# Layer 3's mixing emitted in thirteen shorter steps per group beside the states; narrow heads' turn and division a step apart

## Chip, cores and metric

One Trainium2 chip, one of its cores. The metric is the device time of one execution in microseconds (us), the median of the runs shown. Five engines work side by side, each with an in-order queue of its own: TensorE (PE in the profile, its weight loads PEld), VectorE (DVE), ScalarE (ACT), GpSimd (POOL) and SyncE (SP, which only issues transfers).

## What is computed

The reference is a graph network of four layers over 3125 nodes of 256 features and 50,000 edges. Each layer adds a message-passing block, a mixing block over all nodes and a feed-forward block to x. Three of these matter here, cut to their core:

```python
# layer 2, first graph attention (4 heads of 64), and layer 3's local attention (4 heads of 64)
w = exp(leaky_relu(s[src] + d[dst]) - bound[dst])
out = segment_sum(xW[src] * w, dst) / segment_sum(w, dst)      # then bias, elu, W2 (layer 2)

# layer 3, states: 256 channels x 16 states, nodes in an order by degree
h_t = dA_t * h_(t-1) + dBx_t ;  y_t = sum over states (h_t * C_t)   # then + x*D, * silu(z), @ out_proj

# layer 3, mixing: linear attention of 8 heads, then a small network
msg = layernorm((Q @ KV / (Q @ sumK)) @ Wm)
x + layernorm(relu(concat(x, msg) @ W1) @ W2)                 # W1: 512 x 512, W2: 512 x 256
```

All are 32-bit floats.

## The kernel before

Nodes are cut into 25 tiles of 125. The kernel is one Python class that emits instructions; many of its methods are generators, and a caller advances one generator a step (up to its next `yield`) in order to place its instructions among those of another. The recording layer then lays the instructions out on each engine's queue in an order near to that of emission, but not the same: independent instructions of neighbouring steps are interleaved.

**Narrow heads** (`sums_by_feature`, L1154; called for layer 2's first attention and for layer 3's local attention). Target tiles are taken in four blocks of 7, 6, 6 and 6 tiles (`COLUMNS`, L58). In a block, for each of the 25 source tiles s, a tile of the adjacency is loaded, VectorE makes one product t of 125 x 750 for each of 4 heads (L1209; 875 wide in the first block), and TensorE adds features x t to the sums: L1214 for the numerators, two heads side by side in the two halves of PE's 128 columns, in two chunks of 375; L1223 for the denominators, four heads in groups of 32 columns, emitted for two source tiles at a time. The sums fill six PSUM banks and two more (pool `gf_ps`) are left for everything else. After a block ScalarE copies the sums out (L1231), and each target tile becomes a job (`tile_work`, L1169): TensorE turns its sums with three transposes into `ps_sum` (L1173), and `use` divides them on VectorE (`shares`, L1243 to L1247), adds a bias and applies elu (L1287 to L1291). In layer 2 (`use1`, L1310) further steps turn the tile (x2t, L1318) and multiply it by W2 (ps_h, L166 by way of `product`); in layer 3 (`use`, L1909) the elu ends it. `advance` (L1180), called after every second source tile of the next block, moves every active job by one step, the oldest first, and starts one waiting job. So transposes and division of a tile are emitted in one step. After the last block a loop advances until no job is left.

**States with mixing beside** (`l3_mamba`, L1952). Nodes go in seven groups (`GROUPS`, L57): six of 4 tiles (500 nodes) and one of 1. For each group there are 16 states, and for each state and each half of the channels a fixed chain (`recur`, L2066): TensorE spreads a row of B over the partitions (ps_b, L2073), ScalarE makes da (L2080), VectorE multiplies u by ps_b (L2081) and runs the scan over the 500 nodes (L2082), GpSimd multiplies the result by a row of C (L2085), and TensorE adds it to y through an identity (L2091). State s+1 is emitted ahead of the sum of state s-1. Among the states stand, one step per state, the next group's preparation (`first_part`: input projection, convolution, softplus) and, for the first nine states of a group, one step of `beside`, which is the mixing (`l3_mix`, L1835) together with a search for a maximum (`peak`) whose first 16 steps ride on the mixing's. What is left of `beside` is run out after the last group.

The mixing goes over the same seven groups with weights that are loaded before. A group of 4 tiles takes eight steps: queries; heads; turn; product with Wm; centring; scaled turn; the hidden layer (four chunks, each four matmuls of 500 columns and one Relu on ScalarE); the product with W2 (four tiles, each four matmuls of 256 columns, and a copy on ScalarE). What follows the last one (second centring, gain, sum into X on GpSimd) goes with the next group's first step. The mixing and `peak` have two PSUM banks (pool `m3_ps`), the states the other six. The hidden layer and the outward product are emitted by the helpers `hidden` (L552) and `outward` (L565), which other blocks of the kernel use too.

The slots of a group:

```python
                    if s:
                        next(more, None)
                    if s % 16 < 9:
                        next(beside, None)
```

Of the kernel before, what the change touches and what calls it, by code (L numbers as in the profile page):

```python
# [60 lines left out]
class Net:  # L61
# [487 lines left out]
        nc.scalar.activation(m, m, AF.Exp)  # L549
        nc.vector.scalar_tensor_tensor(out, x, 0.0, m, op0=ALU.max, op1=ALU.add)  # L550

    def hidden(self, psum, out, w1, xt, chunks, func, bias=None, scale=None):  # L552

        nt = xt[0].shape[-1]
        for f in range(chunks):
            ps = psum.tile([128, 512], F32, name="ps_hidden", tag="mm")
            self.product(ps[:, :nt], [w1[:, k, f * 128:(f + 1) * 128] for k in range(len(xt))], xt)
            kw = {}
            if bias is not None:
                kw["bias"] = bias[:, f:f + 1]  # L560
            if scale is not None:
                kw["scale"] = scale[:, f:f + 1]
            self.nc.scalar.activation(out[:, f, :], ps[:, :nt], func, **kw)  # L563

    def outward(self, psum, ht, w2, chunks, n, use, bias=None):  # L565

        for j0 in range(0, n, 2):
            ps = psum.tile([128, 512], F32, name="ps_out", tag="mm")
            for j in range(j0, min(j0 + 2, n)):
                y = ps[:P, (j - j0) * D:(j - j0 + 1) * D]  # L570
                self.product(y, [ht[:, k, j * P:(j + 1) * P] for k in range(chunks)]
                             + ([] if bias is None else [self.ones[:, :P]]),
                             [w2[:, k, :] for k in range(chunks)] + ([] if bias is None else [bias]))
            for j in range(j0, min(j0 + 2, n)):
                use(j, ps[:P, (j - j0) * D:(j - j0 + 1) * D])

    def attention_keys(self, wp, prefix, xnt, biased, banks):

# [575 lines left out]
    def sums_by_feature(self, es, mine, over, h, heads, width, loops, use):  # L1154

        nc = self.nc
        pairs = heads // 2  # L1160
        most = max(n for _, n in COLUMNS) * P
        lp = es.enter_context(self.pool("gf_p", heads + 1))
        ap = es.enter_context(self.pool("gf_a", 4))
        tp = es.enter_context(self.pool("gf_t", 3 * heads + 1))
        op = es.enter_context(self.pool("gf_o", 1))
        cp = es.enter_context(self.pool("gf_acc", 1, PSUM))
        pp = es.enter_context(self.pool("gf_ps", 2, PSUM))

        def tile_work(sums, j, i):  # L1169
            js = slice(j * P, (j + 1) * P)  # L1170
            ps = pp.tile([128, 512], F32, name="ps_sum", tag="mm")
            for k in range(pairs + 1):
                nc.tensor.transpose(ps[:P, k * 128:(k + 1) * 128], sums[:, k, js], self.ident)  # L1173
            num = ps[:P, :heads * width].rearrange("p (h c) -> p h c", h=heads)
            den = ps[:P, heads * width:heads * width + 128].rearrange("p (h c) -> p h c", h=heads)[:, :, 0]
            yield from use(pp, i, (num, den), None) or ()

        waiting, active = [], []

        def advance():  # L1180
            for job in list(active):
                if next(job, self) is self:
                    active.remove(job)
            if waiting:
                job = waiting.pop(0)
                if next(job, self) is not self:
                    active.append(job)

        for i0, n in COLUMNS:
            w = n * P  # L1190
            chunks = ((0, (n + 1) // 2 * P), ((n + 1) // 2 * P, w))
            rows = []
            for hd in range(heads):
                rows.append(lp.tile([P, most], F32, name="rows"))
                self.spread(pp, [(rows[hd][:, b0 * P:b1 * P].rearrange("p (n q) -> p n q", q=P),
                                  [mine[:, i0 + j, hd:hd + 1] for j in range(b0, b1)])
                                 for b0, b1 in ((0, (n + 1) // 2), ((n + 1) // 2, n))])
            acc = [[cp.tile([128, 512], F32, name=f"acc{k}{c}") for c in range(2)] for k in range(pairs + 1)]
            held = []
            for s in range(NT):  # L1200
                a = ap.tile([P, most], F32, name="a")
                self.halves(nc.sync, a[:, :w], self.adj_rows()[s * P:(s + 1) * P, i0 * P:i0 * P + w])
                if loops and i0 <= s < i0 + n:
                    blk = a[:, (s - i0) * P:(s - i0 + 1) * P]
                    nc.vector.tensor_add(blk, blk, self.ident[:P, :P])
                t = []
                for hd in range(heads):
                    t.append(tp.tile([P, most], F32, name="t"))
                    nc.vector.scalar_tensor_tensor(t[hd][:, :w], rows[hd][:, :w], over[:, s, hd:hd + 1],  # L1209
                                                   a[:, :w], op0=ALU.max, op1=ALU.mult)  # L1210
                for k in range(pairs):
                    for c, (c0, c1) in enumerate(chunks):
                        for q in range(2):
                            nc.tensor.matmul(acc[k][c][q * width:(q + 1) * width, :c1 - c0],  # L1214
                                             h[:, s, 2 * k + q, :width], t[2 * k + q][:, c0:c1],
                                             start=(s == 0), stop=(s == NT - 1), skip_group_check=True)
                held.append((s, t))
                if s % 2 == 0 and s < NT - 1:
                    continue
                for s1, t1 in held:  # L1220
                    for c, (c0, c1) in enumerate(chunks):
                        for hd in range(heads):
                            nc.tensor.matmul(acc[pairs][c][hd * 32:(hd + 1) * 32, :c1 - c0],  # L1223
                                             h[:, s1, hd, width:].to_broadcast([P, 32]), t1[hd][:, c0:c1],
                                             start=(s1 == 0), stop=(s1 == NT - 1), skip_group_check=True)
                held = []
                advance()
            sums = op.tile([128, pairs + 1, most], F32, name="sums")
            for k in range(pairs + 1):
                for c, (c0, c1) in enumerate(chunks):  # L1230
                    nc.scalar.copy(sums[:, k, c0:c1], acc[k][c][:, :c1 - c0])  # L1231
            waiting += [tile_work(sums, j, i0 + j) for j in range(n)]
        while waiting or active:
            advance()
# [600 lines left out]
    def l3_mix(self, weights, kvs, pp, xt):  # L1835
# [3 lines left out]
        with ExitStack() as es:  # L1839
            kp = es.enter_context(self.pool("m3"))  # L1840
            for g, n in GROUPS:
                w = n * P
                x = kp.tile([128, KC, 4 * P], F32, name="x")
                nc.sync.dma_start(x[:, :, :w], xt[:, :, g * P:g * P + w])
                xs = [x[:, c, :w] for c in range(KC)]
                att = yield from self.attention_queries(kp, pp, xs, wq, None, kvs, n)
                yield
                y = kp.tile([P, 4, D], F32, name="y")

                def keep(j, ps):  # L1850
                    nc.scalar.copy(y[:, j, :], ps)
                self.outward(pp, att, wm, KC, n, keep)
                yield
                msg = kp.tile([P, 4, D], F32, name="heads")
                self.centred(kp, msg[:, :n, :], y[:, :n, :], n, "n1")
                yield
                mt = kp.tile([128, KC, 4 * P], F32, name="att")
                self.turn_scaled(pp, mt[:, :, :w], msg[:, :n, :], n, g1, c1)
                yield
                h = kp.tile([128, 4, 4 * P], F32, name="h")  # L1860
                self.hidden(pp, h[:, :, :w], w1, xs + [mt[:, c, :w] for c in range(KC)], 4, AF.Relu)
                yield
                self.outward(pp, h, w2, 4, n, keep)
                yield
                msg = kp.tile([P, 4, D], F32, name="heads")
                self.centred(kp, msg[:, :n, :], y[:, :n, :], n, "n2")
                nc.vector.tensor_mul(msg[:, :n, :], msg[:, :n, :], g2[:, None, :].to_broadcast([P, n, D]))
                nc.gpsimd.tensor_add(self.X[:, g:g + n, :], self.X[:, g:g + n, :], msg[:, :n, :])
# [83 lines left out]
    def l3_mamba(self, xs, ys, beside):  # L1952
# [6 lines left out]
        with ExitStack() as es:  # L1959
# [151 lines left out]
            for k, (g, n) in enumerate(GROUPS):  # L2111
# [8 lines left out]
                for s in range(S):  # L2120
# [5 lines left out]
                        next(done, None)  # L2126
                    if s:
                        next(more, None)
                    if s % 16 < 9:
                        next(beside, None)  # L2130
                self.through(more)
                add(S - 1, w, acc, terms[S - 1])
# [433 lines left out]
```

## Time and profile before

| what | us |
|---|---|
| median of 3 runs (6839.69 to 6856.35) | 6845.12 |
| the profiled execution | 6837.53 |
| its span, first to last instruction | 6835.7 |
| layer 2's narrow heads, first sum to last | 3736.1 to 4237.7 |
| states with mixing, first scan to last scan's end | 4986.3 to 5645.1 |
| layer 3's narrow heads, first sum to last | 5675.0 to 6223.5 |

Mean granted TensorE clock over the span: 0.911 of full speed. In the profile, "busy" is the time in which an engine had an instruction in work; a row of a group gives the line, the engine, what it writes and reads, count, busy time, the mean of one, and the engine's idle time ahead of it with what ended it. One fp32 matmul of the program shows as two TensorE instructions ("passes"), one of bf16 as one. Busy tenths of VectorE and TensorE's granted clock over the span, 171 us a digit (the states' stage is digits 30 to 33, the narrow heads 22 to 25 and 34 to 37):

```profile
DVE  7634123216777744115046887546478787776433
```

```profile
PEclk9887998998899999889967999989889988998887
```

### The profile page before, as it was taken

What the parts mean: (1) busy time and instruction counts of PE and PEld (TensorE: products, weight loads), DVE (VectorE), ACT (ScalarE), POOL (GpSimd) and SP (SyncE); (2) the same over time, 40 slices, a digit from 0 to 9 for tenths busy, and PEclk for the clock granted to TensorE, in tenths of its full rate; (3) what the DMA queues carried; (4) which work ended last, traced back from release to release, by engine and by line L of the source; (5) the groups of instructions that cost most, each with busy time, mean ns of one, the idle gap of its engine ahead of it and who ended that gap; (6) DMA issues with size and microseconds to landing.
All of it is one profiled execution on the core that took longest, in us unless ns stands there. A gap on an engine that the chain in (4) does not pass through costs nothing. (4 is left out here: it accounts for less than half of the span.)

```text
span 6835.7 us, 78438 instructions
## 1 busy us (share of the span) xinstructions
PE 5895.7 (86%) x29487; PEld 3956.4 (58%) x29487; DVE 3703.1 (54%) x7628; ACT 1607.7 (24%) x3404; POOL 890.0 (13%) x685
## 2 busy tenths in 40 slices
PE   6887899997799989899946999989778878997775
PEld 5555785564799978668833344776434443333553
DVE  7634123216777744115046887546478787776433
ACT  2433002232011110123323011002356660003411
POOL 0000000003100001400041000120344441001111
PEclk9887998998899999889967999989889988998887
DMA  2634447401122234225510221430331223222132
GB/s 67 107 48 65 120 134 218 139 10 56 54 61 65 60 110 135 63 83 171 167 46 25 79 80 56 138 102 1 92 49 49 53 48 95 65 70 72 43 116 76
DMA packets 421340, 562.01 MB, mean 82 GB/s; under 512 B 120485, under 2 KB 307169, under 8 KB 417153
## 3 DMA queue, kind: packets, MB, share of 16 engines
q1 hardware_dynamic: 353687, 458.72, 25.3%
q10 hardware_dynamic: 40467, 70.52, 3.7%
q0 software_dynamic: 26752, 27.20, 1.5%
q8 instruction: 247, 4.05, 0.2%
q14 instruction: 187, 1.53, 0.1%
HBM read 446.41 MB, written 109.65 MB: 81 GB/s over the span
## 5 line engine op out<-in xcount | busy, mean ns | idle before, releaser
L1134 DVE SCALAR_TENSOR_TENSOR t<-rows,over,a 125x625 f32<-125x625 f32 x750 | 619.7, 866 | 424.3 <-PE acc L1139 417.1
L1209 DVE SCALAR_TENSOR_TENSOR t<-rows,over,a 125x750 f32<-125x750 f32 (+1 forms) x800 | 794.7, 1044 | 56.5 <-PE acc L1223 52.0
L1214 PE MATMUL acc<-t,g_h 125*64 125x375 f32 (+1 forms) x3200 | 625.1, 500 | 12.0 <-DVE t L1209 12.0
L1139 PE MATMUL acc<-g_h,t 125*125 125x129 f32 x5000 | 572.4, 274 | 6.3 <-ACT x L1264 3.5
L1139 PE MATMUL acc<-h,t 125*125 125x257 f32 x2500 | 557.3, 383 | 19.5 <-DVE t L1134 9.7
L1139 PEld LDWEIGHTS acc<-g_h,t 125*125 125x125 f32 x5000 | 563.7, 187 | 11.1 <-DVE t L1134 4.3
L1139 PEld LDWEIGHTS acc<-h,t 125*125 125x125 f32 x2500 | 466.6, 188 | 103.4 <-PE acc L1139 18.9
L1214 PEld LDWEIGHTS acc<-t,g_h 125*64 125x64 f32 x3200 | 226.8, 136 | 356.1 <-issue 245.9
L1223 PE MATMUL acc<-t,g_h 125*32 125x375 f32 (+1 forms) x3200 | 376.8, 496 | 0.0
L2085 POOL TENSOR_TENSOR bx<-h,crow 128x500 f32<-128x500 f32 (+1 forms) x224 | 270.9, 1225 | 342.3 <-DVE h L2082 108.9
L2091 PE MATMUL y<-bx,ident 128*128 128x500 f32 (+1 forms) x448 | 244.1, 655 | 76.3 <-POOL bx L2085 74.5
L771 PE MATMUL agg<-h,a 125*125 125x257 f32 x1250 | 277.9, 382 | 14.3 <-DMA a<-adj 9.0
L837 DVE SCALAR_TENSOR_TENSOR X<-ps_out,prob,X 125x256 f32<-125x256 f32 x200 | 87.9, 479 | 357.1 <-PE ps_out L166 357.0
L771 PEld LDWEIGHTS agg<-h,a 125*125 125x125 f32 x1250 | 233.4, 188 | 57.1 <-issue 18.5
L2082 DVE TENSOR_TENSOR_SCAN h<-da,state,bx 128x500 f32<-128x500 f32 (+1 forms) x224 | 247.1, 1131 | 20.8 <-ACT da L2080 18.4
L1223 PEld LDWEIGHTS acc<-t,g_h 125*32 125x32 f32 x3200 | 104.0, 109 | 248.5 <-issue 247.7
L563 ACT ACTIVATE h<-ps_hidden,L_ffn_b,bn_s 128x500 f32<-128x500 f32 (+1 forms) x224 | 160.7, 723 | 355.0 <-PE ps_hidden L166 329.5
L166 PE MATMUL ps_hidden<-xbt,w 128*128 128x250 f32 x928 | 205.0, 379 | 16.2 <-ACT xbt L151 16.2
L166 PE MATMUL ps_out<-w,hb 128*125 128x256 f32 x928 | 205.0, 379 | 0.0
L166 PEld LDWEIGHTS ps_hidden<-xbt,w 128*128 128x128 f32 x928 | 174.8, 191 | 42.0 <-ACT xbt L151 23.1
L166 PE MATMUL ps_hidden<-XNT,L_ffn_W 128*128 128x500 f32 (+1 forms) x448 | 199.1, 569 | 0.0
L2091 PEld LDWEIGHTS y<-bx,ident 128*128 128x128 f32 x448 | 87.7, 224 | 190.1 <-POOL bx L2085 154.2
(724 smaller groups left out, 9433.6 us busy)
## 6 DMA issues: line engine op xcount, KB each, us to landing
a<-adj SPq DMA_DIRECT2D x500, 273.4 KB
a<-adj SPq DMA_DIRECT2D x150, 328.1 KB
arow<-adj SPq DMA_DIRECT2D x25, 1367.2 KB
adj<-block SPq DMA_DIRECT2D x22, 1531.2 KB
w<-in_L_ffn_W1p SPq DMA_DIRECT2D x29, 1024.0 KB
w<-in_L_ffn_W2p SPq DMA_DIRECT2D x29, 1024.0 KB
crow<-crows ACTq DMA_DIRECT2D x96, 250.0 KB
a<-adj SPq DMA_DIRECT2D x50, 382.8 KB
```

The costliest lines, as they stand in the source:

```text
L166: self.nc.tensor.matmul(ps, lhsT[k], rhs[k], start=(k == 0), stop=(k == n - 1))
L563: self.nc.scalar.activation(out[:, f, :], ps[:, :nt], func, **kw)
L771: nc.tensor.matmul(acc[b][:P, :D + 1], a[:, b * P:(b + 1) * P], h[:, s, :], start=(s == 0), stop=(s == NT - 1))
L837: nc.vector.scalar_tensor_tensor(x, ps, prob[:, g + j, e:e + 1], x, op0=ALU.mult, op1=ALU.add)
L1134: nc.vector.scalar_tensor_tensor(t[:, hd, :], rows[:, hd, :], over[:, s, hd:hd + 1], a, op0=ALU.max, op1=ALU.mult)
L1139: nc.tensor.matmul(acc(b, hd), t[:, hd, b * P:(b + 1) * P], h[:, s, hd, :], start=(s == 0 and first), stop=(s == NT - 1), skip_group_check ...
L1209: nc.vector.scalar_tensor_tensor(t[hd][:, :w], rows[hd][:, :w], over[:, s, hd:hd + 1], a[:, :w], op0=ALU.max, op1=ALU.mult)
L1214: nc.tensor.matmul(acc[k][c][q * width:(q + 1) * width, :c1 - c0], h[:, s, 2 * k + q, :width], t[2 * k + q][:, c0:c1], start=(s == 0), sto ...
L1223: nc.tensor.matmul(acc[pairs][c][hd * 32:(hd + 1) * 32, :c1 - c0], h[:, s1, hd, width:].to_broadcast([P, 32]), t1[hd][:, c0:c1], start=(s1 ...
L2082: nc.vector.tensor_tensor_scan(h[:, :w], da[:, :w], bx[:, :w], state[:, c, s:s + 1], op0=ALU.mult, op1=ALU.add)
L2085: nc.gpsimd.tensor_mul(bx[:, :w], h[:, :w], crow[:, :w])
L2091: nc.tensor.matmul(acc[c][:, :w], self.ident, terms[c][:, :w], start=(s == 0), stop=(s == S - 1))
```

## The change

Four edits. `hidden` and `outward` become generators, `hidden_steps` with a yield after each chunk and `outward_steps` with a yield after each pair of tiles; under the old names thin wrappers run them through, so that their other users emit what they did. In the mixing the hidden layer and the second outward product are taken as steps, so a group of 4 tiles has twelve yields instead of eight (with what follows the last one, thirteen pieces), and `beside` is advanced in the first 13 states of a group instead of the first 9. In the narrow heads `tile_work` yields between its transposes and the division, and `advance` goes through the active jobs from the newest to the oldest.

```diff
+    def hidden(self, *args):
+        self.through(self.hidden_steps(*args))
+
+    def outward(self, *args):
+        self.through(self.outward_steps(*args))
...
             self.nc.scalar.activation(out[:, f, :], ps[:, :nt], func, **kw)
-
-    def outward(self, psum, ht, w2, chunks, n, use, bias=None):
+            yield
+
+    def outward_steps(self, psum, ht, w2, chunks, n, use, bias=None):
...
                 use(j, ps[:P, (j - j0) * D:(j - j0 + 1) * D])
+            yield
...
                 nc.tensor.transpose(ps[:P, k * 128:(k + 1) * 128], sums[:, k, js], self.ident)
+            yield
             num = ps[:P, :heads * width].rearrange("p (h c) -> p h c", h=heads)
...
-            for job in list(active):
+            for job in active[::-1]:
                 if next(job, self) is self:
...
-                self.hidden(pp, h[:, :, :w], w1, xs + [mt[:, c, :w] for c in range(KC)], 4, AF.Relu)
-                yield
-                self.outward(pp, h, w2, 4, n, keep)
-                yield
+                yield from self.hidden_steps(pp, h[:, :, :w], w1, xs + [mt[:, c, :w] for c in range(KC)], 4,
+                                             AF.Relu)
+                yield from self.outward_steps(pp, h, w2, 4, n, keep)
...
-                    if s % 16 < 9:
+                    if s < 13:
                         next(beside, None)
```

More of the change, by code (lines that the diff above doesn't have):

```diff
@@ L550, in positive, with hidden_steps @@
         nc.vector.scalar_tensor_tensor(out, x, 0.0, m, op0=ALU.max, op1=ALU.add)
-    def hidden(self, psum, out, w1, xt, chunks, func, bias=None, scale=None):
+    def hidden(self, *args):
+        self.through(self.hidden_steps(*args))
+    def outward(self, *args):
+        self.through(self.outward_steps(*args))
+    def hidden_steps(self, psum, out, w1, xt, chunks, func, bias=None, scale=None):
         nt = xt[0].shape[-1]
```

## The prediction

> **What bounds the kernel now.** I read the page first, then busy time by stage, then the waits of the stage around the states, and last the order of time on single engines. The page names no one engine:
>
> ```profile
> PE 5895.7 (86%) x29487; PEld 3956.4 (58%) x29487; DVE 3703.1 (54%) x7628; ACT 1607.7 (24%) x3404; POOL 890.0 (13%) x685
> ```
>
> So I cut out the stages that the diff reaches: the narrow heads (4 heads of 64) of layer 2, 3736 to 4267 us, the states with layer 3's mixing, 4982 to 5646, and layer 3's narrow heads, 5675 to 6224. Busy times by stretch (stretch, then PE, PEld, DVE, ACT, POOL, then granted clock):
>
> ```profile
> 3990.00:4113.00 123.00, 122.63 (x872) 50.38 (x870) 102.75 (x145) 13.14 (x38) 0.00 (x0) 1.00 0.28 77
> 4237.70:4267.00 29.30, 16.47 (x51) 10.90 (x51) 11.46 (x36) 9.34 (x29) 0.20 (x1) 0.61 0.00 1
> 4982.00:5646.00 664.00, 553.95 (x1616) 275.03 (x1617) 527.69 (x852) 412.30 (x858) 310.90 (x243) 0.90 0.22 51
> 5953.00:6088.00 135.00, 135.00 (x842) 47.64 (x840) 102.20 (x146) 9.40 (x22) 0.00 (x0) 1.00 0.25 70
> ```
>
> A block of six columns of tiles takes 123 us in layer 2 and 135 in layer 3, TensorE without a gap at full clock in both, VectorE with 20 to 33 us to spare. The two do the same matmuls, and layer 2 has more work per tile. The order of time on TensorE says why layer 3 is slower:
>
> ```profile
> 5989.44 1.49 PE L1214 MATMUL acc<-t,g_h 125*64 125x375 f32 x8
> 5990.86 1.45 PE L1223 MATMUL acc<-t,g_h 125*32 125x375 f32 x6
> 5992.24 1.48 PE L1214 MATMUL acc<-t,g_h 125*64 125x375 f32 x8
> 5993.65 1.46 PE L1223 MATMUL acc<-t,g_h 125*32 125x375 f32 x10
> 5995.03 1.48 PE L1214 MATMUL acc<-t,g_h 125*64 125x375 f32 x4
> ...
> 6067.50 5.28 PE L1214 MATMUL acc<-t,g_h 125*64 125x375 f32 x32
> 6072.71 2.73 PE L1223 MATMUL acc<-t,g_h 125*32 125x375 f32 x32
> 6075.37 5.28 PE L1214 MATMUL acc<-t,g_h 125*64 125x375 f32 x32
> ```
>
> Late in a block, 32 instructions of L1214 take 5.21 us from start to next start and 32 of L1223 take 2.66. Early in it, where tiles are turned and divided, the queue alternates in pieces: eight of L1214 take 1.42 us, but four also 1.41; six of L1223 take 1.38, as ten do. All these fit one rule: a piece costs 0.63 us for each "wave" plus 0.15 us. A wave holds one matmul on each group of PE columns (two groups of 64 in L1214, four of 32 in L1223, two passes each); a piece has as many waves as its fullest group has matmuls. A broken queue therefore pays half-empty waves.
>
> In the states' stage neither engine is full: TensorE 554 of 664 us, VectorE 528. Its waits (engine and line, who released it, total, times, longest) and the order of time on TensorE and then VectorE around one group's hidden layer:
>
> ```profile
> DVE bx L2081 <- PE ps_b L2073: 67.4, 22, 16.7
> DVE h L2082 <- ACT da L2080: 18.4, 14, 4.3
> ```
>
> ```profile
> 5115.87 1.84 PE L166 MATMUL ps_hidden<-x,L_mix_W 128*128 128x500 f32 x4
> ...
> 5127.61 1.84 PE L166 MATMUL ps_hidden<-att,L_mix_W 128*128 128x500 f32 x4
> 5129.29 0.38 PE L2073 MATMUL ps_b<-bc,pick 96*128 96x500 bf16 x1
> ```
>
> ```profile
> 5120.94 4.49 DVE L2028 SCALAR_TENSOR_TENSOR xc<-raw,cw,xc 128x500 f32<-128x500 f32 x6 [2.08 <-ACT xc L2026]
> 5129.70 1.26 DVE L2081 TENSOR_TENSOR bx<-u,ps_b 128x500 f32<-128x500 f32 x2 [4.27 <-PE ps_b L2073]
> ```
>
> The next state's row (ps_b) stands behind 32 passes of the hidden layer, 13.4 us. VectorE, which spends 3.5 us on a state, finishes what it has and stands.
>
> **Part 1: the heads' turn and division a step apart.** No instruction is added. Costs come from where instructions stand in the changed program's queues. I counted waves and pieces in both orders, over the last three blocks of each stage (the first has no tiles to finish and keeps its order). Before, the rule gives 126.9, 123.0 and 121.5 us for layer 2's blocks, up to the next one's first matmul, and 139.8, 134.2, 133.9 for layer 3's; the trace has 125.9, 122.2, 122.2 and 139.3, 134.7, 135.3 for the blocks alone, so I trust it within some 2 us a block.
> - Layer 2: L1214's waves 319 to 306, L1223's 166 to 167, pieces 149 to 142. 12 × 0.63 + 7 × 0.15 = 8.6 us less.
> - Layer 3: L1214's 328 to 310, L1223's 230 to 204, pieces 268 to 240. 44 × 0.63 + 28 × 0.15 = 31.9 us less.
>
> Here a rule of the Trainium skill differs: "TensorEngine Tiling (Array Packing)", section Key Properties, says that changing the tiling mode drains TensorE. By that rule alone the gain would be the switches, (7 + 28) × 0.15 = 5 us. The rows decide: four L1214 instructions of one column half take as long as eight of both, so the half-empty waves cost 0.63 us each, and these are most of the 40 us.
>
> Is TensorE still fed? Per two source tiles VectorE needs eight products at 0.99 us and one tile's division, 9.5 us together; TensorE falls from 11–13.8 to 9.2–11.4. Taking the larger of the two pair by pair gives 31.0 us less in layer 3 and 9.1 in layer 2, so the cover is thin but holds. What waits: the division reads the turned sums, and behind it in VectorE's queue stand the next products, for which TensorE waits. Before, the division stood 0.5 to 1.6 source tiles behind its transposes in most of layer 2, after mostly 2.0: VectorE keeps a longer lead. PSUM's two banks hold the sums a step longer, but the reversed order lets the division free them before an older tile takes the next. Both ends: 28 to 45 us for the two stages; I take 40.
>
> The end of layer 2's heads (the 29 us row above, TensorE 16 busy) is a chain of six tiles, turned sums to turned sums some 4.7 us apart, because each tile's x2t waits for its activation and stands ahead of the next tile's sums. In the new queue the first two sums stand together and each later one stands a tile ahead. A full pairing would save 3 × 4.7 = 14 us, none 0; VectorE's 1.9 us a tile, ScalarE's 1.8 and TensorE's 1.9 remain in line. I take 7. The end of layer 3's heads has the same queue as before: 0.
>
> **Part 2: the mixing in twelve yields instead of eight, states 0 to 12 instead of 0 to 8.** No instruction is added here either; ScalarE's queue loses four table loads. For each of the 112 states I summed what stands on TensorE from its ps_b to the next (0.42 us a pass of 500 columns, 0.22 of 256, 0.215 a ps_b) and what VectorE does per state (rows of the stage, 3.5 us bare), and took the larger. Before: 624 us; the trace has 658 from first to last scan, 1.056 times that. After: 600. In group 1 the old order has states of 16.2 and 10.5 us of TensorE against 7.5 and 4.4 of VectorE, the new one 6.1, 6.9, 6.9, 6.9. The excess of TensorE over VectorE sums to 121 us before (the trace leaves VectorE idle for 136) and 99 after. If queues even out over 2, 4 or 8 states, the difference is 24, 28, 23. So 23.3 × 1.056 = 25 us. Ends: nearly all of the 67 us of ps_b waits (−60), or nothing.
>
> What moves with it: the group's x load on SP's queue moves by one place past another load, no cost; ps_hidden now takes one bank per state, so ScalarE's 0.54 us evacuation no longer holds TensorE; four table loads less are 4 × 1.28 = 5 us of ScalarE, which has 412 of 664 busy: 0. "TensorE: Matmul & The Clock Gate", Part 1, speaks against short bursts: the clock is cut to half when TensorE was lately idle. The stage's row has 0.90 granted. If gaps between the smaller pieces took it to 0.84, the lowest of its 100 us windows, the states bound by TensorE (some 250 us) would take 18 us more, and 7 us would be left of the 25. But the same work in less time makes TensorE busier, so I leave it at 0.
>
> **Sum.** 40 + 7 + 25 = 72 us. The profiled execution took 6837.5 us (span 6835.7): 6766. The median of the runs shown is 6845.1, 7.6 above it: 6773.
>
> **Rivals.**
> - Mixing gives nothing: the time goes to waits on the new neighbours (first_part's convolution and softplus now share states with the mixing). For it: VectorE's 83 us per full group hardly leaves room at the end of a group. 47 us less: 6798. Chance 0.22.
> - Mixing gives most of its ps_b wait, since small pieces are absorbed by one state's lead: 40 + 7 + 58 = 105 less, 6740. Chance 0.15.
> - Little anywhere: VectorE's 9.5 us a pair becomes the heads' bound with its own waits, mixing nothing: 10 us less, 6835. Chance 0.08.
> - Slower: a turned tile's bank is held into the next step, and TensorE, in order, stands at the next x2t or sums of 38 tiles inside the blocks. At the tail's chain of 4.7 us each: +179 − 25, 6999. It decides over 2.4 us a tile, (72 + 20.5) / 38. Against it: the new queue puts each x2t no earlier than its tile's last VectorE step. Chance 0.04.
>
> **How the numbers follow.** Forecast 6773 with 0.51. A measurement tells 0.3%, 20.5 us, from no change. Faster 0.88 (forecast and the first two rivals), same 0.08, slower 0.04. The range runs from the second rival's side, 6735, to 6812, past the first rival with 14 us for the heads' lower bound and the scatter of runs.
>
> **What would show it.** Layer 3's last three blocks at 125–129 us each, layer 2's at 119–123, the tail near 22. The L2081 wait for ps_b under 45 us in total with none near 16, and the stage at some 640 us. Wrong if blocks keep 135 us (the waves are not the cost), if TensorE shows waits at L1318 or L1173 inside blocks, or if VectorE's idle time stays 136 under other names.

## The result and the profile after

| | us | runs |
|---|---|---|
| before | 6842.48 (6839.69 to 6856.35) | 4 |
| changed | 6754.56 (6747.62 to 6762.80) | 4 |

The ratio is 0.9868, 95% interval 0.9849 to 0.9887: 87.9 us less, where 72 were forecast. The profiled execution of the changed kernel took 6747.62 us, its span 6745.8, and its mean granted clock was 0.907. Line numbers have moved: L1214 is now L1223, L1223 is L1232, L2073 is L2081, L2081 is L2089.

The page's row of engines first. The counts of instructions are those of before, but for four table loads on ScalarE:

```profile
PE 5820.6 (86%) x29487; PEld 3940.7 (58%) x29487; DVE 3700.8 (55%) x7628; ACT 1599.3 (24%) x3400; POOL 884.5 (13%) x685
```

TensorE shows 75 us less busy for the same matmuls. Nearly all of it lies in the stages that the diff reaches (some 46 us in the heads and 25 in the states), measured in both traces by the same marks:

| stage | before | changed | difference | forecast |
|---|---|---|---|---|
| layer 2's narrow heads, first sum to last | 501.6 | 487.9 | -13.7 | -8.6 |
| their end, last sum to last W2 copy | 31.7 | 22.7 | -9.0 | -7 |
| states with mixing, first scan to last scan's end | 658.7 | 619.7 | -39.0 | -25 |
| layer 3's narrow heads, first sum to last | 548.5 | 516.1 | -32.4 | -31.9 |

The four differences sum to 94. The spans differ by 90: the code ahead of layer 2's heads, which the diff doesn't touch, took 5 us more in this execution (over the runs of this study it lies between 3729 and 3754). Between and after the stages nothing moved by more than 0.6 us.

Busy time by stretch in the changed kernel (stretch, then PE, PEld, DVE, ACT, POOL, then granted clock): a block of layer 2's heads and a block of layer 3's.

```profile
3991.00:4109.00 118.00, 117.75 (x867) 48.80 (x867) 102.31 (x145) 13.02 (x38) 0.00 (x0) 1.00 0.29 81
5884.00:6009.00 125.00, 125.00 (x837) 44.82 (x836) 102.99 (x146) 8.82 (x21) 0.00 (x0) 1.00 0.27 76
```

The block of layer 3 went from 135 us to 125 with TensorE busy in all of it, before and after, at full clock: what went is not idle time but time inside the matmuls. The order of time on TensorE, early in a block, shows it:

```profile
5911.82 0.82 PE L1232 MATMUL acc<-t,g_h 125*32 125x375 f32 x2
5912.57 1.49 PE L1223 MATMUL acc<-t,g_h 125*64 125x375 f32 x8
5913.99 0.84 PE L1232 MATMUL acc<-t,g_h 125*32 125x375 f32 x8
5914.75 1.49 PE L1223 MATMUL acc<-t,g_h 125*64 125x375 f32 x8
5916.17 2.10 PE L1232 MATMUL acc<-t,g_h 125*32 125x375 f32 x22
```

The queue still alternates, but in fuller pieces: eight instructions of L1232 take 0.76 us from start to next start, which is one full wave (two take 0.75, a wave as well, with three of its four column groups empty). Before, six had taken 1.38. Waves and pieces can be counted along the whole stage.

In the states, one state's row (ps_b) now stands behind one chunk of the hidden layer, 3.35 us, instead of four, 13.4. TensorE's order in the changed kernel:

```profile
5104.89 1.84 PE L166 MATMUL ps_hidden<-x,L_mix_W 128*128 128x500 f32 x4
5106.56 1.84 PE L166 MATMUL ps_hidden<-att,L_mix_W 128*128 128x500 f32 x4
5108.24 0.38 PE L2081 MATMUL ps_b<-bc,pick 96*128 96x500 bf16 x1
```

VectorE's waits in that stage (engine and line, who released it, total, times, longest), changed kernel:

```profile
DVE bx L2089 <- PE ps_b L2081: 54.3, 20, 8.1
DVE h L2090 <- ACT da L2088: 11.5, 12, 4.8
...
DVE n_st L125 <- ACT y L1860: 1.1, 1, 1.1
```

And the row of the same view of before that the prediction left out:

```profile
DVE n_st L125 <- ACT y L1851: 17.6, 7, 5.4
```

The wait for ps_b fell by 13 us only. The larger part of what VectorE no longer waits was for ScalarE: the centring (n_st) waited for ScalarE's copies of the outward product, 17.6 us in all, and now 1.1; da gave 7, the convolution's scaling and the square root of the centring 4 each. The wait for the mixing's heads on TensorE (L650) grew by 5. The whole stage, first scan to last scan's end, before and changed:

```profile
4986.30:5645.10 658.80, 553.06 (x1613) 274.26 (x1613) 527.59 (x850) 410.16 (x856) 310.45 (x242) 0.90 0.21 51
4968.50:5588.10 619.60, 528.39 (x1613) 273.72 (x1613) 524.21 (x850) 401.43 (x851) 303.49 (x242) 0.93 0.23 54
```

VectorE's idle time fell from 131.2 to 95.4 us, 36 of the 39. The granted clock rose as well: by the records of the traces TensorE had half of its clock in 133 us of this stage before and in 91 after, and was busy in 107 and 72 of these. At half clock a pass of the hidden layer took 0.83 us, at full clock 0.42. By an estimate from these numbers (107 less 72, halved) 17 of TensorE's 25 us less busy time are the clock's.

### The profile page after: what moved, and what is told of

Same layout as the page of the kernel before. It is cut to its first block, busy times and chain, and to the rows that moved or that the text cites. A ratio compares the mean times of both kernels' runs of the same rounds, so it can differ in the third digit from the quotient of the medians.

```text
span 6745.8 us, 78396 instructions
## 1 busy us (share of the span) xinstructions
PE 5820.6 (86%) x29487; PEld 3940.7 (58%) x29487; DVE 3700.8 (55%) x7628; ACT 1599.3 (24%) x3400; POOL 884.5 (13%) x685
## 5 line engine op out<-in xcount | busy, mean ns | idle before, releaser
L1223 PE MATMUL acc<-t,g_h 125*64 125x375 f32 (+1 forms) x3200 | 596.0, 500 | 13.0 <-DVE t L1218 13.0
L1147 PEld LDWEIGHTS acc<-h,t 125*125 125x125 f32 x2500 | 466.2, 188 | 103.1 <-PE acc L1147 18.8
L1223 PEld LDWEIGHTS acc<-t,g_h 125*64 125x64 f32 x3200 | 219.7, 136 | 340.6 <-issue 239.1
L1232 PE MATMUL acc<-t,g_h 125*32 125x375 f32 (+1 forms) x3200 | 359.2, 496 | 0.0
L845 DVE SCALAR_TENSOR_TENSOR X<-ps_out,prob,X 125x256 f32<-125x256 f32 x200 | 87.9, 479 | 357.1 <-PE ps_out L166 356.9
L2099 PE MATMUL y<-bx,ident 128*128 128x500 f32 (+1 forms) x448 | 222.2, 610 | 67.4 <-POOL bx L2093 65.4
L779 PEld LDWEIGHTS agg<-h,a 125*125 125x125 f32 x1250 | 234.0, 189 | 57.7 <-issue 18.8
L1232 PEld LDWEIGHTS acc<-t,g_h 125*32 125x32 f32 x3200 | 99.6, 109 | 237.0 <-issue 236.1
L166 PE MATMUL ps_hidden<-xbt,w 128*128 128x250 f32 x928 | 204.9, 379 | 16.2 <-ACT xbt L151 16.2
L166 PEld LDWEIGHTS ps_out<-w,hb 128*125 128x125 f32 x928 | 174.1, 188 | 25.8
```

What stands on the lines that cost most here:

```text
L166: self.nc.tensor.matmul(ps, lhsT[k], rhs[k], start=(k == 0), stop=(k == n - 1))
L779: nc.tensor.matmul(acc[b][:P, :D + 1], a[:, b * P:(b + 1) * P], h[:, s, :], start=(s == 0), stop=(s == NT - 1))
L845: nc.vector.scalar_tensor_tensor(x, ps, prob[:, g + j, e:e + 1], x, op0=ALU.mult, op1=ALU.add)
L1147: nc.tensor.matmul(acc(b, hd), t[:, hd, b * P:(b + 1) * P], h[:, s, hd, :], start=(s == 0 and first), stop=(s == NT - 1), skip_group_check ...
L2099: nc.tensor.matmul(acc[c][:, :w], self.ident, terms[c][:, :w], start=(s == 0), stop=(s == S - 1))
```

## The experiments

My theory had three parts. In the heads, TensorE's queue pays whole waves, and the change cuts their number. At the end of layer 2's heads a chain of turns becomes shorter. In the states, the mixing's lumps stand ahead of ps_b. The rivals: VectorE's lead over TensorE, not the waves, makes the heads faster; the thirteen slots, not the smaller pieces, make the states faster. Stage times of all runs, in the table's marks (us); a stage whose code is that of before came out between 658.0 and 660.9 for the states, and the heads within 2 us. Four runs have the changed mixing (changed, e4_mixing, e8_grouped, e12_grouped); their stage lies between 619.7 and 626.1:

| run | layer 2's heads | end | states | layer 3's heads |
|---|---|---|---|---|
| before | 501.6 | 31.7 | 658.7 | 548.5 |
| changed | 487.9 | 22.7 | 619.7 | 516.1 |
| e1_heads | 487.8 | 22.6 | 660.7 | 517.2 |
| e2_yield | 497.1 | 18.5 | 658.0 | 523.7 |
| e3_newest | 493.4 | 36.3 | 660.9 | 550.1 |
| e4_mixing | 501.6 | 31.7 | 623.8 | 548.9 |
| e5_hidden | 487.9 | 22.7 | 631.6 | 516.0 |
| e6_outward | 487.8 | 22.7 | 659.8 | 516.1 |
| e7_slots | 487.8 | 22.7 | 674.1 | 516.7 |
| e8_grouped | 463.5 | 21.8 | 624.1 | 465.6 |
| e9_grouped_old | 478.6 | 30.5 | 659.2 | 468.1 |
| e10_ahead | 463.6 | 21.8 | 628.0 | 465.3 |
| e11_finer | 463.6 | 21.8 | 650.1 | 465.0 |
| e12_grouped | 463.6 | 21.8 | 626.1 | 465.3 |

### The two halves of the change, each alone

e1_heads keeps the heads' edits; the mixing is as before.

```diff
-                yield from self.hidden_steps(pp, h[:, :, :w], w1, xs + [mt[:, c, :w] for c in range(KC)], 4,
-                                             AF.Relu)
-                yield from self.outward_steps(pp, h, w2, 4, n, keep)
+                self.hidden(pp, h[:, :, :w], w1, xs + [mt[:, c, :w] for c in range(KC)], 4, AF.Relu)
+                yield
+                self.outward(pp, h, w2, 4, n, keep)
+                yield
...
-                    if s < 13:
+                    if s % 16 < 9:
```

> Only the two edits in the narrow heads (the yield behind the transposes, the newest job first). My theory, that the two parts of the change add up: layer 2's narrow heads 488 us from first to last sum and layer 3's 516, as in the changed kernel, the end of layer 2's heads some 9 us shorter than before, the states' stage 659 us as before; 55 us less than the kernel before in all. Rival, that part of the gain needs both edits at once (for instance through the order of the transfers): less than 45 us or more than 65.

e4_mixing keeps the mixing's edits; the heads are as before.

```diff
                 nc.tensor.transpose(ps[:P, k * 128:(k + 1) * 128], sums[:, k, js], self.ident)
-            yield
...
-            for job in active[::-1]:
+            for job in list(active):
```

> Only the mixing's shorter steps in the first 13 states of a group. My theory: the states' stage 620 us from first to last scan as in the changed kernel, the heads 502 and 548 as before; 39 us less than the kernel before. Rival: the stage gains only together with the heads: 650 or more.

e1_heads took 6791.60 us (ratio 0.9924, 0.9908 to 0.9941), e4_mixing 6813.59 (0.9955, 0.9937 to 0.9973), beside 6847.23 for the kernel before. 55.6 and 33.6 us sum to 89, the whole of the change (88) within the intervals: no help or hindrance between the halves shows. Each moved its own stages alone.

### The heads' two edits, each alone

e2_yield is e1_heads with the jobs taken from the oldest to the newest again; e3_newest is e1_heads without the yield between turn and division.

```diff
-            for job in active[::-1]:
+            for job in list(active):
```

> Only the yield between transposes and division, jobs still from the oldest. My theory, that the time of the heads is waves and pieces in TensorE's queue: the queue of this kernel has 316 and 166 waves and 152 pieces in layer 2's last three blocks (before 319, 166, 149) and 316, 206 and 248 in layer 3's (before 328, 230, 268), so layer 2's heads 500 us (502 before) and layer 3's 523 (549 before). Rival, that it is VectorE's lead (the division standing further behind its transposes): the yield gives that alone, so 488 and 516 as in the changed kernel.

```diff
                 nc.tensor.transpose(ps[:P, k * 128:(k + 1) * 128], sums[:, k, js], self.ident)
-            yield
```

> Only the newest job first, transposes and division still in one step. My theory, waves and pieces: 306 and 166 waves and 136 pieces in layer 2, so 486 to 488 us there; layer 3's queue is that of the kernel before, so 548 us. Rival, VectorE's lead: without the yield nothing is gained, 502 and 548.

e2_yield took 6797.63 us and e3_newest 6849.75, one run each. In layer 3 the yield gives 24.8 of the 32.4 us; taking the newest first gives nothing alone and 7.6 on top of the yield. In layer 2 the yield gives 4.5 alone and the order 8.2. At the end the yield alone gives 13.2, more than both together (9.0), and the order alone costs 4.6.

The counts stand beside it. In the last three blocks of a stage (waves of the numerators, waves of the denominators, pieces):

| | layer 2 | layer 3 |
|---|---|---|
| before | 319, 166, 149 | 328, 230, 268 |
| changed | 306, 167, 142 | 310, 204, 240 |
| e2_yield | 316, 166, 152 | 316, 206, 248 |
| e3_newest | 306, 166, 136 | 328, 230, 268 |

For layer 3 the rule gives e2_yield (12 + 24) × 0.63 + 20 × 0.15 = 25.7 us less (measured 24.8) and e3_newest none (measured 1.6 more). Layer 2 doesn't follow it alone: e3_newest, expected at 486 to 488 us by the rule, has as few waves as the changed kernel and is 5.5 us slower. I summed, in these three blocks of each trace, the time from each piece's start to the next piece's. The numerators' pieces take 217.0 us before, 212.2 in e2_yield, 212.1 in e3_newest, 204.9 in the changed kernel; the rule gives 213.6, 211.7, 203.4 and 203.9. So 3.4 us before and 8.7 in e3_newest lie over the rule, with 0.5 and 1.0 where the yield is. The numerators are what waits for VectorE's products. TensorE's matmuls show no idle time for it (some 2 us in each of the four stages), but the other engines' rows do. Inside one of these pieces of e3_newest, 16 instructions that take 3.61 us where others take 2.68:

```profile
3894.87 0.16 DVE L1253 TENSOR_SCALAR share_r<-ps_sum 125x4 f32<-125x4 f32 x1 [2.00 <-PE ps_sum L1181]
3894.95 0.99 DVE L1217 SCALAR_TENSOR_TENSOR t<-rows,over,a 125x750 f32<-125x750 f32 x1
3895.99 0.22 PEld L1222 LDWEIGHTS acc<-t,g_h 125*64 125x64 f32 x2 [0.40 <-DVE t L1217]
```

VectorE stands 2.00 us at the division for the turned sums, the product behind it ends at 3895.94, and the weight load that needs it starts 0.05 us later. The product for the other column half ends 0.97 us after that one, so the rest of the piece runs one half after the other instead of both side by side. The waits at the division and for products in layer 2's last three blocks, e3_newest and then e2_yield (engine and line, who released it, total, times, longest):

```profile
DVE share_r L1253 <- PE ps_sum L1181: 34.6, 17, 7.3
PEld acc L1222 <- DVE t L1217: 23.9, 65, 0.6
DVE share_r L1254 <- PE ps_sum L1181: 4.1, 1, 4.1
PEld acc L1223 <- DVE t L1218: 16.0, 45, 0.6
```

So in layer 2 the yield also keeps VectorE from standing at the division, and the few us over the rule go with that.

### Does the queue's order cost what the rule says? Waves kept whole

If half-empty waves are the cost, a queue without broken pieces must be faster still, and on the old kernel too. e8_grouped is the changed kernel with the denominators' matmuls tied, in the order of issue, behind the numerators of their source tiles, and the next numerators behind these denominators. No instruction is added.

```diff
+    def behind(self, done):
+        return ExitStack() if done is None else self.tc.issue_after(done.ins)
...
-            held = []
+            held, before = [], None
...
-                for k in range(pairs):
...
+                with self.behind(before):
+                    for k in range(pairs):
...
+                                top = nc.tensor.matmul(acc[k][c][q * width:(q + 1) * width, :c1 - c0],
...
-                for s1, t1 in held:
...
+                with self.behind(top):
+                    for s1, t1 in held:
...
+                                before = nc.tensor.matmul(
```

> The changed kernel with TensorE's queue of the narrow heads fixed: the numerators' matmuls of a source tile may not be queued ahead of the denominators' emitted before them, and the other way round, so that pieces are not broken. In its queue 306 and 150 waves and 90 pieces in layer 2's last three blocks (306, 167, 142 in the changed kernel), 312, 150 and 106 in layer 3's (310, 204, 240); TensorE's sum 457 and 442 us against 482 and 498. My theory, waves and pieces until VectorE binds (448 us of work in each stage and its standing at the sums): layer 2's heads 465 to 475 us, layer 3's 455 to 475, 55 to 80 us less than the changed kernel. Rival: pieces cost nothing by themselves, since VectorE's products set the pace and TensorE was filling its waiting time with pieces: 488 and 516 as in the changed kernel, or more, because TensorE now waits for the fourth head's product.

e9_grouped_old makes the same edit on the kernel before, with none of the change in it.

> The kernel before with the same fixed queue, none of the change. 319 and 150 waves, 100 pieces in layer 2's last three blocks; 312, 150 and 121 in layer 3's. My theory, waves and pieces: layer 2's heads 475 to 485 us (502 before), layer 3's 460 to 480 (549 before), without any change of how far the division stands from its transposes. Rival, VectorE's lead: 502 and 548 or more.

e8_grouped took 6665.03 us in one run. TensorE's order in a block of layer 3 there (L1227 are the numerators, L1238 the denominators):

```profile
5855.99 2.73 PE L1238 MATMUL acc<-t,g_h 125*32 125x375 f32 x32
5858.65 5.28 PE L1227 MATMUL acc<-t,g_h 125*64 125x375 f32 x32
...
5866.52 0.59 PE L1184 MATMUL ps_sum<-ident,sums 128*125 128x128 f32 x3
```

and the busy times of a block of layer 3:

```profile
5836.00:5946.00 110.00, 110.00 (x842) 46.35 (x842) 102.09 (x146) 9.37 (x22) 0.00 (x0) 1.00 0.30 86
```

The denominators stand in pieces of 32 and the numerators are broken only by the tiles' own work. A block takes 110 us in layer 3 instead of 135 and 125, and VectorE, 102 busy, is now close behind. e9_grouped_old, 6741.97 us in one run beside 6846.63 for the kernel before, has 468.1 in layer 3 where that kernel has 548.5. By the counts that were expected and the rule, layer 3 should lose (16 + 80) × 0.63 + 147 × 0.15 = 82.5 us against the kernel before and 52.9 from changed to e8_grouped; it lost 80.4 and 50.5. With whole waves the change's edits are worth 2.5 us there. So in layer 3 they worked through the waves, and VectorE's lead as the main cause is refuted. In layer 2 the same pair is 478.6 and 463.5. There tying the queue alone doesn't make all waves whole: the last three blocks have 319, 150 and 100 (waves, waves, pieces) in e9_grouped_old, 306, 150 and 90 in e8_grouped, where 300 and 150 are the fewest that the matmuls need. By the rule these counts differ by 13 × 0.63 + 10 × 0.15 = 9.7 us. Of the other 5, the tiles' own short pieces give 2.6, and the rest lies in the numerators' pieces beyond the rule.

e12_grouped is e8_grouped again, for an interval.

> e8_grouped once more, now timed beside the others on one chip. By the first look, 0.973 of the kernel before (0.970 to 0.976); the stages within 2 us of the first look.

It took 6675.51 us beside 6844.75 for the kernel before: ratio 0.9751, 0.9736 to 0.9766. It is faster than both kernels, by 169 us and, from the two ratios, by about 80.

### The states: which piece, or the slots?

e5_hidden cuts the hidden layer only and leaves the outward product whole, in 12 slots a group; e6_outward cuts the outward product only, in 10; e7_slots cuts neither and keeps the 13 slots.

```diff
-                yield from self.outward_steps(pp, h, w2, 4, n, keep)
+                self.outward(pp, h, w2, 4, n, keep)
+                yield
...
-                    if s < 13:
+                    if s < 12:
```

> The changed kernel with the outward product of the mixing whole again (one step of four tiles) and the hidden layer in four steps, 12 states of a group with a mixing step. Theory A, that the gain of the states' stage is the hidden layer that stands ahead of the next state's ps_b: the stage 620 to 628 us from first to last scan, the waits for ps_b near 54 us in total. Theory B, that a good half is the outward product whose copies on ScalarE hold the centring and with it VectorE's queue (n_st waiting for y: 17.6 us before, 1.3 after): 636 to 642 us, n_st's wait for y back at 15 us or more.

```diff
-                yield from self.hidden_steps(pp, h[:, :, :w], w1, xs + [mt[:, c, :w] for c in range(KC)], 4,
-                                             AF.Relu)
+                self.hidden(pp, h[:, :, :w], w1, xs + [mt[:, c, :w] for c in range(KC)], 4, AF.Relu)
+                yield
...
-                    if s < 13:
+                    if s < 10:
```

> The changed kernel with the hidden layer of the mixing whole again and the outward product in two steps, 10 states of a group with a mixing step. Theory A (the hidden layer ahead of ps_b): the stage 650 to 659 us, ps_b waits 67 us with single ones of 13 us or more. Theory B (half is the outward product's copies): 636 to 642 us, n_st's wait for y under 4 us.

```diff
-                yield from self.hidden_steps(pp, h[:, :, :w], w1, xs + [mt[:, c, :w] for c in range(KC)], 4,
-                                             AF.Relu)
-                yield from self.outward_steps(pp, h, w2, 4, n, keep)
+                self.hidden(pp, h[:, :, :w], w1, xs + [mt[:, c, :w] for c in range(KC)], 4, AF.Relu)
+                yield
+                self.outward(pp, h, w2, 4, n, keep)
+                yield
```

> The changed kernel with both products of the mixing whole again (eight steps for a group, as before), but still advanced in the first 13 states of a group. My theory, that the shorter pieces make the gain of the states' stage and not the slots: the sum over the states of the larger of TensorE's and VectorE's work is 629 us (624 before, 600 in the changed kernel), so the stage 655 to 668 us, ps_b waits 65 us or more. Rival, that spreading over 13 states is the gain: 620 to 640 us.

The runs took 6756.79, 6773.26 and 6814.65 us, one each, and the stage 631.6, 659.8 and 674.1. The hidden layer alone gives 27 us, the outward product alone nothing, both together 33 to 39 (619.7 to 626.1 in the four runs). e5_hidden lies between the ranges that its two theories named. VectorE's waits in the stage, e5_hidden:

```profile
DVE bx L2090 <- PE ps_b L2082: 50.1, 20, 9.4
DVE h L2091 <- ACT da L2089: 12.7, 12, 4.0
DVE n_st L125 <- ACT y L1860: 11.0, 4, 4.8
```

e6_outward:

```profile
DVE bx L2089 <- PE ps_b L2081: 79.4, 20, 17.3
DVE h L2090 <- ACT da L2088: 18.2, 13, 4.3
...
DVE n_st L125 <- ACT y L1860: 3.3, 2, 2.1
```

In e6_outward the wait for the copies is gone, 17.6 to 3.3, and the wait for ps_b has grown from 67.4 to 79.4, with one of 17.3: one wait took the other's place. With a lump of 13.4 us ahead of ps_b, the shorter steps behind it gave VectorE nothing that it could use. With the lump cut, cutting the outward product as well is worth another 6 to 12 us, and the copies' wait of 11.0 in e5_hidden is 1.1. The wait for da went with the hidden layer: 12.7 in e5_hidden, 18.2 in e6_outward. Part of the 6 to 12 us may be the clock's: TensorE's granted clock in the stage is 0.90 in e5_hidden and 0.91 to 0.93 in the four runs.

e7_slots is slower than the kernel before, by 15 us in the stage, which neither reading had. With eight pieces and 13 slots the mixing runs ahead of the states: its hidden layers are spent by the fifth group instead of the sixth. The first five groups of states take 569 us against 532 before, the last two 105 against 126. So it packs lumps closer; it shows that more slots with whole pieces give no gain, but it is no clean test of the slots in themselves. VectorE waited 52.5 us for ps_b there, less than before, but 29.3 for the copies.

### What the rest of the wait for ps_b is

54 us of it are left. Either ps_b is emitted too late, and a longer lead removes it, or TensorE's pieces are still too large. e10_ahead is e8_grouped with ps_b and da emitted two states ahead instead of one.

```diff
-                terms = [recur(0, g, w, bc, dt, u)]
+                terms = [recur(0, g, w, bc, dt, u), recur(1, g, w, bc, dt, u)]
...
-                    if s + 1 < S:
-                        terms.append(recur(s + 1, g, w, bc, dt, u))
+                    if s + 2 < S:
+                        terms.append(recur(s + 2, g, w, bc, dt, u))
```

> The kernel with the fixed queue of the narrow heads (e8_grouped), and each state's chain emitted two states ahead instead of one, so that ps_b of state s+2 stands ahead of the mixing's step of state s. My theory, that what is left of VectorE's waiting is ps_b behind one step of the mixing: its 54.7 us fall below 30 and the stage goes from 624 to 590 to 605 us. Rival, that a longer lead only moves the wait (two ps_b banks are all that the states have, so the preparation's matmuls wait for a bank, or the y sums' bx buffers run out): 615 us or more. In all 6630 to 6645 us by the first, 6655 to 6675 by the second.

e11_finer is e8_grouped with each hidden chunk in two steps of two matmuls, so that a group takes 16 steps in 16 slots.

```diff
+                        if k == 1:
+                            yield
+                    nc.scalar.activation(h[:, f, :w], ps[:, :w], AF.Relu)
+                    yield
...
-                    if s < 13:
+                    if s < 16:
```

> e8_grouped with the mixing cut finer still: each hidden chunk of four matmuls in two steps, 16 steps a group, one in every state. If the size of the piece ahead of ps_b is what counts: ps_b waits below 45 us, the stage 600 to 612 us (624). If it is how TensorE's and VectorE's work is balanced state by state: that sum is 600 us as before, with one state of 13.7 us, and the stage 618 to 630 us.

e10_ahead took 6678.14 us (0.9747, 0.9733 to 0.9760), the stage 628.0 against 624.1 and 626.1 in the two runs of e8_grouped: no gain. Its wait for ps_b is 49.2 us, hardly less than 54. But the trace shows that the edit hardly made the lead longer where it counts: from the end of ps_b to the first product that reads it there are 1.6 us in the median of the 112 states, 1.5 in e8_grouped, and ps_b still stands right behind a whole hidden chunk (passes from 5081.83, ps_b at 5085.18). In its expectation the two banks that ps_b shares with the preparation were the rival; TensorE's waits for such a bank at ps_b are 6.2 us, 2.8 in e8_grouped. So earlier emission gave nothing, and whether a truly longer lead would stays open. e11_finer, 6719.39 us in one run, is 25 us slower in the stage, above both ranges that were named for it. VectorE's waits there:

```profile
DVE bx L2104 <- PE ps_b L2096: 34.0, 17, 4.6
DVE h L2105 <- ACT da L2103: 26.9, 17, 4.1
DVE n_st L125 <- ACT y L1867: 23.9, 13, 3.6
```

The wait for ps_b fell to 34 as the theory of size said, and the stage grew all the same, since 37 us of waits for ScalarE came back (da from 12.1 to 26.9, n_st from 1.1 to 23.9). It is not the clock, which is 0.93 there. Two things differ from e8_grouped, and I tried them only together. The pieces are finer; and with 16 pieces to 16 slots the mixing no longer moves one slot ahead per group, so each group's centring meets the same states. The waits for the copies fall nearly all at two places, ahead of the scans of the first state (9.9 us in all) and of the fifth (13.0). That points to the place and not to the size, but which of the two it is stays open.

## Why the prediction was right, and where its sizes were off

All four terms were forecast too small, by 0.5 to 14 us; no errors cancelled.

**The waves.** Right, and the size too where they are the whole story: layer 3's heads 31.9 forecast, 32.4 measured, and the blocks at 127.4, 125.4 and 123.9 us, inside the 125 to 129 named but for the last. The rival in which TensorE stands 4.7 us at each of 38 tiles did not come: the blocks are shorter, and TensorE is busy in all of 125. That the gain is TensorE's own is shown by e9_grouped_old, which reaches 468 us by the queue's order alone. The page "TensorEngine Tiling (Array Packing)" of the Trainium skill, section Key Properties, would have given some 5 us for both stages by its drains, an estimate with the 0.15 us a piece of the traces; 46 were measured.

**Layer 2's heads.** Mis-sized: 8.6 forecast, 13.7 measured. The blocks lie at 121.1, 117.8 and 117.7, the last two under the 119 to 123 named. By the sums over pieces the term lacked two things: 2.4 us that the numerators took beyond the rule, and 2.6 us in the short pieces of the tiles' own work (transposes 10.2 to 9.2, x2t 5.7 to 5.1, W2 18.8 to 17.8), which the count held constant. The prediction had noted that VectorE keeps a longer lead, but took it only as cover that must hold and gave it no price; what it missed is VectorE's standing at the division, 31.9 us over these blocks before and 16.1 after.

**The end of layer 2's heads.** 7 forecast, 9.0 measured; the end is 22.7 long, 22 was named. My reason was incomplete: I laid the gain to sums standing a tile ahead in the new queue, which is what both edits make together, but the yield alone gives 13 and the reversed order takes 4 of these back. Why it does is not shown.

**The states.** Right in direction and mis-sized: 25 forecast, 39 measured (35 in e4_mixing, 35 in e8_grouped and 33 in e12_grouped, so some 4 to 6 of the 39 are this trace's own). The term that failed is the sum over states of the larger of TensorE's and VectorE's work. It knows two engines. It fell by 24 us, but in the trace only 13 us of ps_b's wait went, 54.3 are left where I had named under 45, and it was ScalarE's side that gave the rest: n_st 16.5, da 7, the square root and the scaling 4 each. ScalarE looked free at 412 us of 664, and I had put its part at 0. What counted was not how busy it is but its place in a short chain: TensorE's product, ScalarE's copy, VectorE's centring. With the product in one step its copies were still under way when the centring came up one step later; with the product in two steps they were done.

**The clock.** The stage's granted clock is 0.93 after 0.90. The fall that the Trainium skill's "TensorE: Matmul & The Clock Gate", Part 1, let one fear from short pieces did not come. Taking it at 0 was safe, but left out a gain: TensorE's time at half clock fell from 133 to 91 us, to 102 to 107 in the three other runs with the changed mixing, whose stage is the 4 to 6 us longer. How much of the stage's gain is the clock's, and how much of the clock is the shorter waits', no run separates.

**The rivals.** "Mixing gives nothing" is refuted by e4_mixing, "little anywhere" by e1_heads. "Most of the ps_b wait goes", priced at 58 us, has the right sign and 39 us instead of 58, most of it by other waits than it named.

## What to carry to other kernels

Where matmuls share TensorE by groups of columns, look at the order of its queue and not only at its busy time: a queue that is busy nearly throughout at full clock held 103 us in the heads of the kernel before that tying matmuls of one shape together in issue order took out, more than the whole change did. Cut the largest lump ahead of the operand that a serial chain waits for, and then read which wait comes next: here the second cut gave nothing without the first, and 6 to 12 us after it. A sum of work per step over two engines is not enough if a third one stands in a chain between them, however idle that one is.

## What the hardware showed beyond that

- A piece of four numerator instructions on one half of PE's columns takes 1.41 us, as long as eight on both halves (1.42), and two of the denominators' take 0.75 as eight do (0.76). The cost of an interleaved queue can be counted from the order alone, to some 3 us a block of 125 (e3_newest's layer 2 is the worst, 8.7 us over the rule in three blocks).
- TensorE's trace shows almost no idle time (some 2 us or less of some 500) in layer 2's stages of before and of e8_grouped, which differ by 38 us for the same matmuls; the lost time is inside the durations.
- Grouping the queue brought layer 3's block to 110 us with VectorE 102 us busy in it. By these busy times its products and the tiles' divisions come next as the bound; no run tests it.
